# A planner's ranks and operation lengths set anew in a six-sublayer transformer kernel

## The chip, the cores and the metric

The kernel runs on one core of one Trainium2 chip. A core has five engines with a queue of instructions each: TensorE (PE: matrix products and transposes; PEld is its loading of the stationary operand), VectorE (DVE), ScalarE (ACT: functions from a table, and copies), GpSimd (POOL), and SyncE (SP), which here issues nearly all plain DMAs. Each engine works through its own queue strictly in order; semaphores tie the queues together. The metric is the device time of one execution in microseconds (us); less is better.

## The reference, cut to what matters

x is 16 sequences of 256 tokens with 128 channels. Two layers of one shape follow each other: half of an FFN, attention, half of the same FFN again.

```python
x = x + 0.5 * L0_ffn(layernorm(x))      # 8 experts of 128 -> 128 -> 128, top 2, SiLU gate, plus one shared expert
x = x + L0_attn(layernorm(x))           # 16 heads of 8; softmax(q1 k1) - lamb * softmax(q2 k2), then a layernorm
x = x + 0.5 * L0_ffn(layernorm(x))
x = x + 0.5 * L1_ffn(layernorm(x))      # 8 experts of 128 -> 256 -> 128, top 2, GELU gate
x = x + L1_attn(layernorm(x))           # 16 heads of 8, causal softmax, output projection
x = x + 0.5 * L1_ffn(layernorm(x))
```

Everything is float32.

## The kernel before

**Tiles.** The 4096 tokens are eight blocks of 512 (`x0` to `x7`), which stay on the chip from load to store. An FFN sublayer is done in parts of two blocks (the very last sublayer ends with two parts of one block each). The first two blocks of the first sublayer go through all experts densely (`dense_expert`), while the machinery of the sparse parts is set up; every other part is sparse. For a sparse part, `gate_block` normalizes and takes the gate, `dispatch` works out on DVE and PE which row goes to which slot, `scatter` writes the rows into `slots_x` in DRAM by indirect DMAs from POOL, `load_tiles` has SP fetch slots (`xg`) and expert weights (`wt`), `compute` does two tiles of 128 slots at a time, `combine` gathers the results `slots_y` by indirect DMAs into `g`, and `add_to_x` adds them on DVE.

**The chain of `compute`.** PE transposes `xg` into a PSUM half bank; ACT or DVE copies it to `xT`; PE multiplies by the first weights into a PSUM tile `big`; ACT applies SiLU or GELU with a bias, giving `s`; DVE multiplies, giving `h`; PE multiplies by the second weights; DVE adds a bias, giving `y`; SP stores `y`.

**Attention.** `Attention.pair` runs units: PE makes scores `big<-q,k`, ACT exponentiates them into `ex` (SiLU, GELU and Exp stand in different tables of ACT, and a change of table is an instruction of its own, ACT_TABLE_LOAD), in layer 1 DVE or POOL masks, PE sums `ex` with `vaug`, ACT copies `avs`, PE transposes it, DVE copies `oall`; `end` normalizes. PSUM has three `big` tiles and, once the dense work is over, four half banks.

**The order.** No engine's order is written by hand. Every piece of work is a generator that asks for an engine, with what it reads, writes and needs of buffers. A planner (`Tasks.run`) runs while the program is built. It keeps a model of time (`Clocks`), starts again and again the request whose modelled start plus `HASTE` (0.003) times its rank is least, and books a modelled length for each instruction (`Timed.book`). The order in which it starts requests becomes the order of PE, ACT, DVE and SP (`ORDERED`). So nothing but the orders follows from its numbers: the data, the shapes and the amount of PE work stay what they are. The same requests may fall to ACT or DVE (`move`) and, for masks, DVE or POOL (`MASKERS`).

**Its numbers.** `FFN_RANK` has a line for each FFN sublayer with a rank for each part; `ATT_RANK` a line for each attention sublayer with a rank for each block; a rank of 100 more is worth 0.3 us of modelled delay. `TABLE` (2.0 us) is added in the choice where ACT would have to change its table. `LATE_ROWS` is what `transfers` adds to the landing time of an indirect DMA (`s + 2.3 + LATE_ROWS`); consumers of `slots_x` and of `g` are planned after it. `Clocks.SEEN` adds 0.18 us between ACT's or DVE's end and another engine's start, 0.25 us after PE.

Nearly every instruction of the profile stands at L136, the line that records it (`f(*args, **kw)` in `Timed`), so groups are told apart by tiles. L1100 issues the scatters, L1258 the gathers. A choice at run time (`bounded`) takes the first of two programs with these inputs; the second, for large scores, is not run.

Of the kernel before, what the change touches and what calls it, by code (L numbers as in the profile page):

```python
# [24 lines left out]
SYNC = mybir.DependencyInfo(mybir.DependencyClass.Sync, mybir.DependencyReason.DATA)  # L25
TABLE = 2.0
LATE = 1.5
LATE_ROWS = 2.0
MARGIN = {"PE": 1.0, "ACT": 1.0, "DVE": 1.5, "POOL": 1.25, "SP": 2.0}
HASTE = 0.003  # L30

FFN_RANK = [
    [65, 53, 99],
    [190, 217, 235, 251],
    [218, 230, 258, 290],
    [420, 438, 430, 453, 403],
]
ATT_RANK = [
    [82, 122, 109, 110, 131, 132, 158, 159],
    [319, 320, 368, 341, 408, 369, 383, 574],  # L40
]


def cols(ap):
    n = 1
    for s in ap.shape[1:]:
        n *= s
    return n
# [6 lines left out]
class Clocks:  # L55
# [52 lines left out]
    def book(self, engine, length, reads, writes, by=None, end=None, start=None, apart=False):  # L108
        s = self.start(engine, reads, () if apart else writes)
        if start is not None:  # L110
            s = max(s, start)
        self.free[engine] = s + length
        end = s + length if end is None else end(s)
        by = by or engine
        for ap in reads:
            for k in self.keys(ap):
                self.read[k] = max(self.read.get(k, (0.0, by)), (end, by))
        for ap in writes:
            for k in self.keys(ap):
                self.wrote[k] = max(self.wrote.get(k, (0.0, by)), (end, by))  # L120
                if self.pending.get(k):
                    self.pending[k] -= 1
        return s


class Timed:
# [19 lines left out]
    def book(self, op, out, ins, args, kw):  # L146
        c, n = self.clocks, max(cols(v) for v in [out, *ins])
        if op == "dma_start":
            size = 4e-6 * n * out.shape[0]
            start = c.start("SP", ins, [out])  # L150

            def end(s):
                c.bytes_free = max(c.bytes_free, s + 1.2) + size / 0.3
                return max(s + 2.2, c.bytes_free + 1.0) + LATE

            c.book("SP", 0.45, ins, [out], by="DMA", end=end, start=start)
        elif self.name == "PE":
            turns = 1 if op == "transpose" or ins[0].dtype == BF else 2
            lanes = 4 if 32 in (out.shape[0], ins[0].shape[0]) else 1
            length = max(max(cols(out), 120) * 0.00094 / lanes, 0.0007 * cols(ins[0]))  # L160
            c.book("PE", turns * length + c.turn, ins, [out])
            c.turn = 0.0
        elif self.name == "ACT":
            func = args[2] if op == "activation" else None
            length = 0.16 + 0.00076 * cols(out)
            if func in (AF.Exp, AF.Silu, AF.Gelu) and func != c.table:
                c.table = func
                length += 1.3
            c.book("ACT", length, ins, [out])
        elif self.name == "DVE":  # L170
            c.book("DVE", 0.145 + 0.00097 * n, ins, [out])
        else:
            c.book("POOL", 0.35 + 0.17 * n if ALU.pow in args else 0.2 + 0.0021 * n, ins, [out])

# [78 lines left out]
def kernel(ctx: ExitStack, tc: tile.TileContext, a: dict, out: bass.AP):  # L253
# [690 lines left out]
    def transfers(todo, when=None, pool=None):  # L944
# [3 lines left out]
        for i in range(0, len(todo), 2):  # L948
# [3 lines left out]
            for j, (issue, _) in enumerate(two):  # L952
                start = clocks.start("POOL", reads)
                dma, ins, o = issue(taken[j] if pool else None)
                if clocks.last_before(start - 1.0) is not None:
                    tc.add_manual_dep(dma.ins, clocks.last_before(start - 1.0).ins.name, SYNC, reason="pace")
                clocks.book("POOL", 1.26, ins, [o], by="DMA", end=lambda s: s + 2.3 + LATE_ROWS, start=start, apart=True)

# [737 lines left out]
```

## Time and profile before

| what | value |
|---|---|
| median of 14 runs | 1536.83 us (1531.57 to 1544.52) |
| the profiled execution | 1524.25 us, of it the span 1522.5 us |
| PE busy | 1248.2 us, 82% of the span |
| PEld, DVE, ACT busy | 838.4, 888.1, 867.3 us (55%, 58%, 57%) |
| POOL busy | 609.6 us (40%) |
| mean granted clock of TensorE | 0.915 |
| HBM traffic | 155 GB/s over the span |

The profiled execution was 0.8% below the median. Busy shares are means over stages of different kinds: in the first 152 us (loads, dense experts, first dispatch) and the last 80 us (last FFN parts, last gathers and stores) PE has the most idle time; in between, FFN parts and attention blocks of different sublayers run beside each other. A "busy" PE may run at half rate; the granted clock tells of that. Where one row of the profile gives a mean for "one", that is from its start to its end; instructions of ACT and DVE that follow each other overlap in part, so several in a row take less than their number times the mean.

### The profile page before, as it was taken

To read this page: it belongs to the slowest core of one execution; us is meant where nothing else is said; L and a number is where in the kernel's file an instruction comes from. 1 tells how busy PE (TensorE), PEld (TensorE's weight loads), DVE (VectorE), ACT (ScalarE), POOL (GpSimd) and SP (SyncE) were. 2 spreads that over 40 slices of the span, in tenths; PEclk is the share of its full clock that TensorE was granted. 3 is DMA by queue.
4 is the path that set the end of the run, shared out by engine and by line. 5 is a ranking of instruction groups with operands and counts; after the bars stand their busy time and mean duration, and the time that the engine had idled before them with its cause. 6 is when DMAs were issued, how large, how long until landed. Compare 5 with 4: busy or idle time off the path is not lost. (4 is left out here: it accounts for less than half of the span.)

```text
span 1522.5 us, 29022 instructions
## 1 busy us (share of the span) xinstructions
PE 1248.2 (82%) x9730; PEld 838.4 (55%) x9730; DVE 888.1 (58%) x3146; ACT 867.3 (57%) x1612; POOL 609.6 (40%) x618
## 2 busy tenths in 40 slices
PE   5958889888898899888889877787878878887772
PEld 3434555554345444456665765476567756656772
DVE  4376734555535366554665676677665557766643
ACT  2114677677667676577678546464456655553431
POOL 2014442240530134424245364637553356475334
PEclk8858999999999999999999999799899989989986
DMA  5356555442125101357456554565355665446882
GB/s 116 96 131 193 181 163 159 148 141 81 49 84 143 32 19 41 116 177 249 139 154 187 188 174 133 179 223 191 136 188 162 204 204 176 138 171 209 269 289 86
DMA packets 207530, 232.85 MB, mean 153 GB/s; under 512 B 32062, under 2 KB 151545, under 8 KB 207371
## 3 DMA queue, kind: packets, MB, share of 16 engines
q1 hardware_dynamic: 192010, 199.42, 42.9%
q0 software_dynamic: 15360, 31.49, 6.3%
q8 instruction: 79, 1.29, 0.3%
q14 instruction: 81, 0.66, 0.1%
HBM read 183.84 MB, written 52.75 MB: 155 GB/s over the span
## 5 line engine op out<-in xcount | busy, mean ns | idle before, releaser
L136 ACT ACTIVATE ex<-big 128x1024 f32<-128x1024 f32 (+1 forms) x384 | 349.1, 958 | 81.5 <-PE big L136 66.6
L1100 POOL DMA_INDIRECT slots_x<-xn,idx x240 | 238.9, 995 | 256.4 <-PE bank L136 56.9
L1258 POOL DMA_INDIRECT g<-slots_y,idx x240 | 239.6, 999 | 241.2 <-PE big L136 61.5
L136 PE MATMUL big<-q,k 32*128 32x512 f32 (+1 forms) x1536 | 259.8, 635 | 14.0 <-ACT ex L136 3.6
L136 PE MATMUL big<-xT,wt 128*128 128x128 f32 x1452 | 205.4, 289 | 17.7 <-ACT xT L136 6.6
L136 ACT ACT_TABLE_LOAD x150 | 192.4, 1283 | 29.9 <-PE big L136 19.6
L136 PE MATMUL bank<-ex,vaug 128*32 128x256 f32 (+1 forms) x3072 | 190.0, 378 | 23.4 <-issue 10.1
L136 PEld LDWEIGHTS big<-xT,wt 128*128 128x128 f32 x1452 | 187.1, 202 | 33.5 <-issue 11.7
L136 POOL TENSOR_TENSOR rstd<-rstd,mhalf 128x4 f32<-128x4 f32 (+1 forms) x64 | 62.5, 977 | 310.7 <-DVE rstd L136 309.8
L136 PEld LDWEIGHTS bank<-ex,vaug 128*32 128x32 f32 x3072 | 92.7, 113 | 104.5 <-issue 37.2
L136 ACT ACTIVATE s<-big,wt 128x128 f32<-128x128 f32 x363 | 107.1, 374 | 67.0 <-PE big L136 34.5
L136 DVE SCALAR_TENSOR_TENSOR h<-big,wt,s 128x128 f32<-128x128 f32 x363 | 104.4, 342 | 60.0 <-ACT s L136 47.7
L136 PE MATMUL bank<-wt,h 128*128 128x128 f32 x726 | 120.2, 304 | 22.3 <-issue 6.6
L136 PEld LDWEIGHTS bank<-wt,h 128*128 128x128 f32 x726 | 102.3, 210 | 50.3 <-issue 17.8
L136 PEld LDWEIGHTS big<-q,k 32*128 32x128 f32 x1536 | 82.1, 193 | 83.8 <-issue 43.0
L136 PE MATMUL big<-xT,rw 128*128 128x128 f32 x720 | 113.7, 299 | 13.4 <-ACT ex L136 8.0
L136 DVE SCALAR_TENSOR_TENSOR x<-g,wgt,x 128x128 f32<-128x128 f32 x240 | 85.4, 360 | 53.0 <-DMA g<-slots_y,idx 40.3
L136 DVE COPY oall<-bank 128x144 f32<-128x144 f32 x96 | 29.2, 305 | 146.1 <-PE bank L136 92.7
L136 PEld LDWEIGHTS big<-xT,rw 128*128 128x128 f32 x720 | 101.5, 212 | 22.0 <-ACT ex L136 10.8
L136 ACT COPY avs<-bank 128x256 f32<-128x256 f32 x96 | 36.0, 375 | 132.4 <-PE bank L136 60.6
L136 DVE TENSOR_TENSOR y<-bank,wt 128x128 f32<-128x128 f32 x235 | 58.9, 284 | 86.4 <-PE bank L136 38.8
L136 ACT COPY xT<-bank 128x256 f32<-128x256 f32 (+1 forms) x184 | 63.2, 373 | 79.0 <-PE bank L136 49.1
(190 smaller groups left out, 1766.6 us busy)
## 6 DMA issues: line engine op xcount, KB each, us to landing
wt<-wcat SPq DMA_DIRECT2D x128, 450.0 KB
rw<-wcat SPq DMA_DIRECT2D x63, 450.0 KB
wt<-wcat SPq DMA_DIRECT2D x107, 257.0 KB
slots_y<-y SPq DMA_DIRECT2D x168, 128.0 KB
rw<-wcat SPq DMA_DIRECT2D x54, 257.0 KB
xg<-slots_x SPq DMA_DIRECT2D x43, 256.0 KB
cwb<-slots_x SPq DMA_DIRECT2D x33, 256.0 KB
slots_x<-zero SPq DMA_DIRECT2D x12, 384.0 KB
```

The lines of the kernel that those rows point to most:

```text
L136: r = f(*args, **kw)
L1100: s = bare.gpsimd.indirect_dma_start(out=self.sx[:, :], out_offset=bass.IndirectOffsetOnAxis(ap=self.idx[:, j, c : c + 1], axis=0), in_=ro ...
L1258: s = bare.gpsimd.indirect_dma_start(out=g[:, :], out_offset=None, in_=self.sy[:, :], in_offset=bass.IndirectOffsetOnAxis(ap=self.idx[:, j ...
```

## The change

Three things in the planner change, and nothing else:

```diff
-LATE_ROWS = 2.0
+LATE_ROWS = 2.5
 FFN_RANK = [
-    [65, 53, 99],
-    [190, 217, 235, 251],
-    [218, 230, 258, 290],
-    [420, 438, 430, 453, 403],
+    [65, 53, 101],
+    [190, 217, 235, 229],
+    [218, 230, 260, 290],
+    [420, 428, 420, 488, 450],
 ]
 ATT_RANK = [
-    [82, 122, 109, 110, 131, 132, 158, 159],
-    [319, 320, 368, 341, 408, 369, 383, 574],
+    [162, 192, 189, 65, 211, 212, 238, 154],
+    [312, 365, 366, 339, 398, 377, 382, 542],
 ]
...
         elif self.name == "ACT":
-            length = 0.16 + 0.00076 * cols(out)
+            length = max(0.25 if cols(out) > 64 else 0.15, 0.055 + 0.00084 * cols(out))
...
         elif self.name == "DVE":
-            c.book("DVE", 0.145 + 0.00097 * n, ins, [out])
+            if op == "reciprocal":
+                length = 0.05 + 0.0084 * n
+            else:
+                length = 0.085 + 0.001 * n + (0.05 if op in ("scalar_tensor_tensor", "bn_stats") else 0.0)
+            c.book("DVE", length, ins, [out])
```

The ranks change for both layers; the modelled length of ACT's copies and activations changes (a copy of 256 columns from 0.355 to 0.27 us), that of DVE's operations too (a tensor_tensor of 128 columns from 0.269 to 0.213 us, a reciprocal of 64 columns from 0.207 to 0.588 us); and indirect DMAs are taken to land 0.5 us later. The model of PE is left as it was.

## The prediction

> **What bounds the kernel now.** I read first the page's busy shares and slices, then the busy time by stage, then who ended the waits, then the groups.
>
> ```profile
> span 1522.5 us, 29022 instructions
> PE 1248.2 (82%) x9730; PEld 838.4 (55%) x9730; DVE 888.1 (58%) x3146; ACT 867.3 (57%) x1612; POOL 609.6 (40%) x618
> PEclk8858999999999999999999999799899989989986
> ```
>
> PE is busy 82% of the span, no other engine over 58%. PE idles 1522.5 - 1248.2 = 274 us; the stages (first 152 us: busy 109.84; from 1440 on, 82.5 us: busy 42.69) put 42 of it in the start and 40 in the end, and 192 in the 1288 us between. A second loss is the rate: by the clock's records TensorE had half rate for 258 us, 198 of them with PE busy; between 152 and 1440 that is 139 busy us, which at full rate would take half, so up to 69 us. The recorded rates are 0.5 and 1.0 only; the page's tenths are means.
>
> I cut PE's busy time into twentieths of 62.4 us of work each, and read the stages that these are:
>
> ```profile
> core 0: us, PE busy (x) PEld busy (x) DVE busy (x) ACT busy (x) POOL busy (x), PEclk, DMA share, GB/s
> 311.00:385.00 74.00, 62.86 (x511) 36.98 (x511) 44.11 (x158) 56.81 (x89) 23.55 (x25) 0.98 0.33 99
> 385.00:454.00 69.00, 62.16 (x564) 26.98 (x560) 28.95 (x100) 43.97 (x62) 31.57 (x33) 0.95 0.23 72
> 454.00:526.00 72.00, 62.63 (x522) 36.82 (x511) 33.71 (x108) 52.72 (x84) 4.46 (x5) 0.98 0.31 88
> 526.00:592.00 66.00, 62.53 (x572) 29.68 (x571) 43.24 (x161) 47.53 (x67) 23.95 (x25) 1.00 0.09 28
> 592.00:664.00 72.00, 62.57 (x477) 34.37 (x469) 38.40 (x134) 42.61 (x71) 29.86 (x31) 0.95 0.32 103
> 958.00:1038.00 80.00, 62.07 (x487) 48.92 (x484) 54.84 (x192) 43.19 (x93) 42.47 (x42) 0.87 0.64 201
> ```
>
> The same PE work takes 66 us where attention is nearly alone (526 to 592), and 80 where FFN parts, dispatch and attention are mixed (958 to 1038). So no single engine or transfer sets the middle; it is short waits of PE for ACT and DVE, whose number depends on the order:
>
> ```profile
> PE bank L136 <- ACT avs L136: 26.1, 20, 3.1
> PE bank L136 <- DVE y L136: 23.9, 24, 3.0
> PE bank L136 <- ACT xnT L136: 19.1, 25, 2.3
> PE big L136 <- ACT ex L136: 17.2, 20, 2.8
> PE bank L136 <- ACT xT L136: 11.5, 15, 2.7
> ```
>
> (us in total, times, longest.) The largest of these are one-copy hand-offs: PE, a copy on ACT, PE.
>
> **The change, part by part.** The two programs' orders on each engine were compared, instruction by instruction. Work is the same: PE 5258 recorded operations in both, SP 721 transfers in both, the same scatters and gathers; 3 of 485 ACT copies go to DVE, one mask from DVE to POOL (730 and 1330 ns: nothing, POOL is idle 60%). What differs is order, and with it the table loads. The change does not give the planner TensorE's half rate; the title's half rate went into the choice of ranks only, so the orders are still planned for full rate.
>
> (1) *Table loads.* The order of ACT has 150 in the program run before and 128 after.
>
> ```profile
> L136 ACT ACT_TABLE_LOAD x150 | 192.4, 1283 | 29.9 <-PE big L136 19.6 <-issue 7.1 <-PEq L1682 0.8
> ```
>
> 22 x 1283 ns = 28.2 us less on ACT. ACT is idle 43%, so most is hidden. From the start of a load to 1 us after its end PE idled 51.4 us over the 150, 0.34 us a load and no larger a share (15%) than elsewhere. Bounds: 0 and 22 x 0.34 = 7.5 us. I take 5, toward the full price, as these loads go where ACT is busiest (311 to 385: 56.81 of 74 us). Without the cover of ACT's idle time they would be worth all 28.2.
>
> (2) *Gathers planned 0.5 us later.* Until 1495 us, when the last gathers begin (their 16 at 1.26 us each follow in both orders alike: block 7's eight, then block 6's), DVE stood at the head of its queue for a gather:
>
> ```profile
> DVE x L136 <- DMA g<-slots_y,idx: 24.4, 24, 2.3
> ```
>
> 24 waits x 0.5 = 12 us of DVE at best. What stands behind is whatever DVE has next (y, h, oall); PEld waited 5.5 us, 6 times, for these additions. Bounds 0 and 5.5; I take 2, by the PE waits' half that 0.5 us of a wait's mean 1.0 us removes, less some for work that now comes after.
>
> (3) *Right lengths.* Rows and timeline: an ACT copy of 256 takes 382 ns alone, two in a row 0.65 us, so the next starts 0.27 us later; before it was planned as 0.355, now 0.27. Of DVE, two y additions take 0.49 us, 0.21 us apart (planned 0.269, now 0.213); a reciprocal of 64 columns 552 ns (0.207, now 0.588). The new numbers are the trace's. PE waited for ACT's avs, xnT, xT (twice, 11.5 and 8.2 us) and k 86 times, 73 us: 86 x 0.085 = 7.3 us, and for y 24 x 0.056 = 1.3 us, if every consumer moves up by the error: bounds 0 and 8.6. I take 4, half, since a consumer moves up only where nothing else was put before it.
>
> ```profile
> L136 ACT ACTIVATE s<-big,wt 128x128 f32<-128x128 f32 x363 | 107.1, 374 | 67.0 <-PE big L136 34.5 <-issue 13.8 <-PE bank L136 12.1
> L136 ACT COPY xT<-bank 128x256 f32<-128x256 f32 x168 | 59.9, 382 | 78.5 <-PE bank L136 48.9 <-issue 12.2 <-DVE y L136 6.5
> ```
>
> Four activations of 128 take 1.14 us, 0.255 each in a row against 374 alone. [...]
>
> (4) *Regrouped layer 0.* Attention of layer 0 is moved by ranks 70 to 80 later, blocks 3 and 7 excepted. In the orders, with each PE operation weighted by its row's busy time, twentieths 5 to 9 (20% to 45%) held 34, 31, 28, 34, 25 Exp and 12, 8, 16, 1, 18 SiLU; now 40, 34, 35, 27, 32 Exp and 0, 1, 8, 17, 4 SiLU. Before, two of the five had under 10 SiLU (385 to 454 and 526 to 592: PE idle 6.8 and 3.5 us, mean 5.2), the other three 11.1, 9.4 and 9.4 (mean 10.0). Now four are of the quiet kind: 2 x 4.8 = 9.6 us, 16 if all four become like the best (40.2 before, 4 x 3.5 + 10.0 after). SP's fetches, POOL's gathers and the FFN work move with it to 45% to 60%: the price of that is in (5). Bounds 0 and 16; I take 10.
>
> (5) *Closer hand-offs.* For each PE step that waits on ACT or DVE I took the PE work that stands between it and the PE step that feeds its chain, the queues' order included. Under 2 us: 303 steps before, 351 after; under 1 us: 105 and 117. Of the 48 more, 24 lie between 45% and 60% of PE's work; the second products (`bank<-h`) rise most, and behind one stand an activation and a multiplication (1.14 and 1.12 us). Over the 18 twentieths between the ends, PE's idle time in the trace grows by 0.39 us with each hand-off under 2 us, or by 0.82 with each under 1 (correlations 0.58 and 0.61). 47 x 0.39 = 18.3 (one of the 48 is in the first twentieth) or 12 x 0.82 = 9.8. Bounds 0 and 18.3; I take 10, since (3) says that part of the slack given up was never needed.
>
> Idle PE also lowers the rate. Between 152 and 1440 us half rate costs up to 69 us beside 192 idle, 0.36 for each us idle; on the net sum that is under 4 us, left in the range. TensorE: Matmul & The Clock Gate (HAM oscillation) has the rule "no PE-idle gaps >~3.4µs": by it waits of at most 2 us cost no rate. Before its last matmul the trace has four stretches that long, one of them past 152 us, and between 152 and 1440 us 147 us of half rate; the measurement decides.
>
> Sum: -5 - 2 - 4 - 10 + 10 = -11 us on the profiled execution's 1524.25, 1513. That one lay 12.6 us below the median of the runs, so the forecast is put on the median: 1536.8 - 11 = 1526 us.
>
> **The rivals.** *The closer hand-offs decide (slower).* Place: 45% to 60% of PE's work, where FFN parts of both layers now meet. If regrouping only carries idle time there, (4) is 0, and (5) is 18.3; with 5 for the table loads, and (2) and (3) lost in the same waits, +13, 1550 us. It decides from a price of 11 / 47 = 0.23 us a hand-off when (4) is 0. For it: the 0.39 of the twentieths, and that 877 to 1114 is already the worst stretch; against it: a copy needs under 1 us, so most hand-offs of 1 to 2 us fit. *All terms at their good end.* -7.5 - 5.5 - 8.6 - 16 = -37.6, half of it with (5) at half (9) gives about -28, with the rate 1507 us. For it: 69 us of half rate and 192 idle to take from; against it: from the second layer's attention on the order of stages is nearly the old one (each begins and ends within 2% of PE's work). *Hidden.* The waits change places and the total stays: 1537 us. For it: start, end and half the middle are nearly unchanged.
>
> **How the numbers follow.** Forecast (1517 to 1532) 0.34, the good end 0.19, no change 0.13, slower 0.34. About 0.3%, 4.6 us, is what a measurement can tell. Faster 0.53, same 0.13, slower 0.34. The bounds, -37.6 and +18.3, are 1499 and 1555; the range that leaves two in ten out is 1502 to 1553. My own range for the forecast alone is 1517 to 1532.
>
> **What would show it.** 128 table loads (if not, (1) falls); gather waits of DVE before the last gathers under 15 us; PE waits for avs, xnT, xT under 60 us in place of 65; PE idle between 20% and 45% of its work near 30 us in place of 40; between 45% and 60% not above 40 (it was 26). If that last stretch gains more than 20 us of idle time, or the mean clock falls below 0.90, the forecast is wrong.

## The result, and the profile after

The changed kernel takes 1596.96 us (median of 10 runs, 1588.64 to 1602.47) against 1535.36 us for the kernel before (47 runs), a ratio of 1.0398 (95% interval 1.0375 to 1.0422). It is slower by 4%. The forecast was 1526 us, and the range ended at 1553. The profiled execution took 1582.8 us, of it 1581.1 us span, 58.6 us more than the span before.

The page of the kernel after, with the busy time of each engine and the granted clock by slices:

```profile
span 1581.1 us, 28975 instructions
PE 1266.0 (80%) x9730; PEld 846.3 (54%) x9730; DVE 891.6 (56%) x3148; ACT 839.9 (53%) x1587; POOL 608.4 (38%) x619
PEclk8859999999999999999998987899889999979986
```

The work is the same 9730 products. PE idles 315.1 us in place of 274.3 (+40.8), and is busy 17.8 us longer: it had half rate for 236 busy us in place of 198, and half of those 38 extra us is the 17.8 to within about a microsecond. So 40.8 of idle time and 17.8 of rate make up the 58.6. ACT is busy 27 us less and DVE 3.5 us more; no engine has become the bound. The table loads are the 128 that were read off the orders:

```profile
L136 ACT ACT_TABLE_LOAD x128 | 164.2, 1283 | 30.4 <-PE big L136 13.7
```

Next the waits of the kernel after (us in total, times, longest), those of PE that answer to the ones shown of before, and DVE's wait for gathers:

```profile
DVE x L136 <- DMA g<-slots_y,idx: 55.5, 51, 6.0
PE bank L136 <- DVE y L136: 37.6, 29, 4.6
PE bank L136 <- DVE h L136: 25.2, 17, 6.2
PE big L136 <- ACT ex L136: 19.8, 24, 2.5
PE bank L136 <- ACT avs L136: 18.4, 15, 4.4
PE bank L136 <- ACT xnT L136: 16.8, 23, 2.6
PE bank L136 <- ACT xT L136: 14.9, 18, 2.3
```

and from the same view of the kernel before one row that the prediction did not show:

```profile
PE bank L136 <- DVE h L136: 7.6, 7, 1.7
```

PE's waits for ACT, summed over all rows of PE's own view, stay at 99 us (before 100). Those for DVE grow from 88 to 137 us, +49, which is more than all the added idle time. The two rows to look at are `y` (23.9 to 37.6) and `h` (7.6 to 25.2): the two DVE steps of the expert chain, with longest waits now of 4.6 and 6.2 us where none was over 3.0.

Where in the run? Cut into twentieths of PE's work (by the weighted orders, as in (4) of the prediction), with PE's idle time beside, the stages changed their length so:

| share of PE's work | longer by, us | idle before, after |
|---|---|---|
| 0 to 10% | -3.9 | 46.7, 47.3 |
| 10 to 20% | +21.5 | 15.3, 28.8 |
| 20 to 35% | -21.5 | 28.1, 13.7 |
| 35 to 45% | +9.6 | 11.6, 19.9 |
| 45 to 60% | +25.1 | 24.7, 42.3 |
| 60 to 80% | +20.0 | 63.1, 74.4 |
| 80 to 100% | +8.0 | 84.8, 88.9 |

The view of windows of the kernel after shows both sides: two of the quiet stages, then the stretch at 50 to 60% of the work, where FFN parts of both layers now meet.

```profile
core 0: us, PE busy (x) PEld busy (x) DVE busy (x) ACT busy (x) POOL busy (x), PEclk, DMA share, GB/s
403.00:463.00 60.00, 57.13 (x528) 24.71 (x528) 30.29 (x93) 44.41 (x62) 5.30 (x6) 1.00 0.00 1
463.00:524.00 61.00, 57.09 (x527) 25.97 (x519) 26.45 (x83) 44.30 (x60) 17.30 (x18) 1.00 0.20 66
735.00:809.00 74.00, 60.52 (x485) 47.23 (x488) 41.81 (x173) 46.21 (x90) 33.28 (x35) 0.95 0.67 211
809.00:894.00 85.00, 66.21 (x499) 42.63 (x497) 44.44 (x158) 47.84 (x87) 47.37 (x49) 0.88 0.55 170
```

The kernel before had these windows for the same shares of the work as the last two:

```profile
726.00:797.00 71.00, 62.18 (x489) 44.38 (x481) 47.94 (x190) 49.27 (x90) 22.45 (x24) 0.93 0.47 142
797.00:864.00 67.00, 59.59 (x530) 40.77 (x527) 40.44 (x143) 48.00 (x85) 29.34 (x29) 0.97 0.70 216
```

A twentieth of the work is 57 us at full clock, so the first two are near the best there can be; the stretch from 809 on takes 85 us where 67 did, at a clock of 0.88 in place of 0.97, with DVE and ACT busy about half of it. It lacks no engine and no bandwidth; things wait in line.

How a closer hand-off costs PE its time can be seen in one place. The timeline of the kernel after (start, duration, engine, and in brackets the idle time before and who ended it), PE first:

```profile
185.82 0.75 PE L136 MATMUL bank<-wt,h 128*128 128x128 f32 x4
186.40 1.88 PE L136 MATMUL big<-xnT,sw 128*128 128x512 f32 x4
192.83 1.22 PE L136 MATMUL bank<-sw,h 128*128 128x128 f32 x4 [4.55 <-DVE y L136]
```

and ACT and DVE in the same stretch:

```profile
190.30 0.69 ACT L136 ACTIVATE s<-big,b_0t 128x512 f32<-128x512 f32 x1
189.68 0.31 DVE L136 COPY oall<-bank 128x144 f32<-128x144 f32 x1 [2.27 <-PE big L136]
189.91 0.74 DVE L136 SCALAR_TENSOR_TENSOR h<-big,b_0t,s 128x512 f32<-128x512 f32 x1
190.57 0.68 DVE L136 TENSOR_TENSOR x<-x,sb 128x512 f32<-128x512 f32 x1
191.17 0.42 DVE L136 TENSOR_TENSOR eq<-lg 128x256 f32<-128x256 f32 x1
191.62 0.42 DVE L136 TENSOR_TENSOR eq<-eq,earlier 128x256 f32<-128x256 f32 x1
191.96 0.42 DVE L136 TENSOR_TENSOR gt<-lg 128x256 f32<-128x256 f32 x1
192.30 0.48 DVE L136 TENSOR_TENSOR y<-bank,wt 128x128 f32<-128x128 f32 x2
```

The product that stands, a second product of the shared expert (`bank<-sw,h`), does not wait for the first one just ahead of it (`big<-xnT,sw`): that one's activation only begins at 190.30, and the `h` that the waiting product reads is from an earlier one and is ready at 190.65. By its program it waits for `y`, which has to read the result of `bank<-wt,h` (185.82) out of the same PSUM bank. Between `bank<-wt,h` and the product that needs its `y` done, PE has 1.88 us of work of its own. DVE is idle until 189.68, and then has a copy, a multiplication for `h`, an addition to `x` and three comparisons of `dispatch` ahead of that `y`. PE stands 4.55 us. In the kernel before, this second product never waited more than 1.24 us; its three groups around 185 us stood behind score products or a dispatch product, which gave PE something to do.

### The profile page after: what moved, and what is told of

Its sections match the earlier page's. It is cut to its first block, busy times and chain, and to the rows that moved or that the text cites. A ratio compares the mean times of both kernels' runs of the same rounds, so it can differ in the third digit from the quotient of the medians.

```text
span 1581.1 us, 28975 instructions
## 1 busy us (share of the span) xinstructions
PE 1266.0 (80%) x9730; PEld 846.3 (54%) x9730; DVE 891.6 (56%) x3148; ACT 839.9 (53%) x1587; POOL 608.4 (38%) x619
## 5 line engine op out<-in xcount | busy, mean ns | idle before, releaser
L1262 POOL DMA_INDIRECT g<-slots_y,idx x240 | 235.4, 981 | 230.6 <-PE bank L136 99.6
L136 PE MATMUL big<-xT,wt 128*128 128x128 f32 x1460 | 215.4, 295 | 21.5 <-ACT ex L136 10.0
L136 PEld LDWEIGHTS big<-xT,wt 128*128 128x128 f32 x1460 | 196.4, 209 | 39.5 <-issue 15.3
L136 POOL TENSOR_TENSOR rstd<-rstd,mhalf 128x4 f32<-128x4 f32 (+1 forms) x64 | 63.3, 988 | 330.1 <-DVE rstd L136 328.9
L136 ACT ACT_TABLE_LOAD x128 | 164.2, 1283 | 30.4 <-PE big L136 13.7
L136 PE MATMUL bank<-wt,h 128*128 128x128 f32 x730 | 124.8, 307 | 29.7 <-issue 8.1
L136 PEld LDWEIGHTS bank<-wt,h 128*128 128x128 f32 x730 | 105.5, 212 | 56.8 <-issue 19.0
L136 DVE SCALAR_TENSOR_TENSOR x<-g,wgt,x 128x128 f32<-128x128 f32 x240 | 89.2, 377 | 63.3 <-DMA g<-slots_y,idx 55.5
L136 POOL TENSOR_TENSOR ex<-ex,causal 128x512 f32<-128x512 f32 x48 | 61.9, 1310 | 105.4 <-ACT ex L136 105.3
```

The source lines that it names most:

```text
L136: r = f(*args, **kw)
L1262: s = bare.gpsimd.indirect_dma_start(out=g[:, :], out_offset=None, in_=self.sy[:, :], in_offset=bass.IndirectOffsetOnAxis(ap=self.idx[:, j ...
```

## The experiments

Three sets of numbers changed (ranks, lengths, `LATE_ROWS`), so the first runs took them apart. The theories, by the letters used in the expectations: A, the new ranks are the cause; B, the new, mostly shorter lengths place each consumer too close behind its producer; C, the order before is one that was selected, and any other order that the planner makes loses (C': loses only on some chips); D, the time follows the count of close hand-offs, that is, of PE steps with under 2 us of PE work between them and the step that feeds their chain (before 303, after 351); E, the new lengths of DVE are shorter than the true ones; F, the fewer table loads are bought with late activations.

The runs were spread over five sessions. In two of them, as in the first comparison, the kernel before took 1536 to 1539 us; in the other three, 1438 to 1441. Ratios are each to the kernel before beside it; the two settings are taken up in the last section. The first four expectations give times for a kernel before of 1535 us, but their session had 1441: only their ratios can be compared.

**One part at a time.** e1_ranks takes only the rank tables of the change, e2_lengths only the lengths of ACT and DVE, e3_late only `LATE_ROWS`, e4_ranks_lengths all but `LATE_ROWS`. Of each part a line, in the order e3, e2, e1:

```diff
-LATE_ROWS = 2.0
+LATE_ROWS = 2.5
...
-            length = 0.16 + 0.00076 * cols(out)
+            length = max(0.25 if cols(out) > 64 else 0.15, 0.055 + 0.00084 * cols(out))
...
-    [82, 122, 109, 110, 131, 132, 158, 159],
+    [162, 192, 189, 65, 211, 212, 238, 154],
```

> The new ranks alone; lengths and the landing time of indirect DMAs as before. The whole change took 61.6 us more at the median (1535.4 to 1597.0). Theory A (ranks were fitted to the new lengths and regroup layer 0 badly; they are the cause): 1580 to 1610 us. Theory B (the shorter planned lengths make the planner place consumers too close; ranks are harmless): 1525 to 1545 us. Theory C (any new order loses, since the old one is a lucky one among many): 1550 to 1590 us, and the lengths alone as much.

> The new lengths of ACT and DVE alone, old ranks. Theory A: 1525 to 1545 us. Theory B: 1580 to 1610 us, with more waits of PE for DVE's h and y than before. Theory C: 1550 to 1590 us.

> Indirect DMAs planned 0.5 us later alone. Theories A and B: 1525 to 1545 us, no difference from before. Theory C: even this small step, which reorders only what stands near a scatter or a gather, loses 10 us or more: 1545 to 1590 us.

> The whole change but for the later landing of indirect DMAs. Theories A and B: within 10 us of the whole change, 1587 to 1607 us. Theory C: anywhere between 1550 and 1600 us, not predictable from the parts.

| kernel | median us | ratio, 95% interval | close hand-offs | table loads |
|---|---|---|---|---|
| before | 1440.98 | 1 | 303 | 150 |
| e1_ranks | 1486.27 | 1.031, 1.026 to 1.037 | 340 | 143 |
| e2_lengths | 1520.79 | 1.054, 1.047 to 1.060 | 365 | 135 |
| e3_late | 1474.08 | 1.023, 1.018 to 1.028 | 331 | 156 |
| e4_ranks_lengths | 1592.35 | 1.106, 1.098 to 1.115 | 387 | 124 |

Every part loses by itself, and the loss grows with the count of close hand-offs. Neither A nor B alone can be the cause: a change of one constant that only delays modelled gathers (e3) loses 2.3%. That asked for a neutral change.

**Neutral changes.** c1_before is the kernel before under another name, c2_after the whole change; n1_haste_up and n2_haste_down alter only the weight of all ranks by 3%, to 0.0031 and 0.0029:

```diff
-HASTE = 0.003
+HASTE = 0.0031
```

> The kernel before, unchanged, for its profile on the same chip as the others of this call. The chip of the last four runs took 1441 us for it and the chips before it 1535. All theories: ratio 1.00. If the time is near 1440 again, its profile shows which instructions, waits or transfers are shorter than in the 1522.5 us profile.

> The whole change, unchanged, on the same chip as the kernel before. Theory C' (the loss of a new order is specific to the chip): the ratio differs clearly from the first comparison's 1.040, and lies near 1.10 on a chip where the kernel before takes 1440 us. Theories A and B: 1.04 on any chip.

> A neutral reshuffle: HASTE 0.0031 in place of 0.003, all else as before. The planner's lengths and ranks are unchanged and the weight of rank grows by 3%, so no theory of a better or worse model predicts anything: A and B 0.995 to 1.005. C (the order before is a lucky one, any reshuffle loses): 1.01 to 1.04.

> The opposite neutral reshuffle: HASTE 0.0029; the first 1600 rows or so of TensorE's order stay as before. A and B: 0.995 to 1.005. C: 1.01 to 1.03.

Beside 1536.43 us: c1_before 1.000 (0.996 to 1.004), c2_after 1.034 (1.027 to 1.041), n1_haste_up 1.020 (1.013 to 1.026), n2_haste_down 1.013 (1.007 to 1.019). A nudge in either direction, which has no better or worse side, costs 1.3 to 2.0%: theory C holds on another chip too (and the whole change, with 1.034, is near the first 1.040, so C' falls for this setting). But the whole change costs more than a nudge, and it is there that PE's waits for DVE rise: all rows together 96 us in c1_before, 92 and 103 in the two nudges, 134 in c2_after.

**The count by itself.** If D is the rule, ranks chosen for the count alone must do well or badly. o1_fewer moves nine ranks of the kernel before so as to have 288 close hand-offs; o2_after_fewer moves twelve ranks of the changed one and has 311 in place of 351; d1_more is o1 with four other ranks (468, 460, 371, and 225 for 217) and has 375; n3_late_down has `LATE_ROWS` at 1.9, and 330. Most of o1's moves:

```diff
-    [420, 438, 430, 453, 403],
+    [420, 453, 445, 453, 433],
-    [319, 320, 368, 341, 408, 369, 383, 574],
+    [319, 320, 369, 341, 423, 367, 383, 604],
```

> Lengths and landing time as before; ten ranks moved, chosen by the order alone so that fewer TensorE steps have under 2 us of TensorE work between them and the step that feeds their chain: 288 in place of 303 (under 3 us: 594 for 603). Theory D (the time follows the number of close hand-offs at 0.6 to 1.3 us each, as in the seven orders run so far): 10 to 20 us faster, ratio 0.987 to 0.994. Theory C (the order before was chosen on the chip among many, and the count only happens to follow): slower, 1.01 to 1.03, like any other reshuffle.

> The whole change with its own lengths and landing time, but ten ranks moved so that 311 hand-offs are under 2 us in place of 351 (under 3 us: 639 for 664); 124 table loads of this kind of order stay few. Theory D: 25 to 50 us faster than the whole change, ratio to before 1.005 to 1.02. Theory B (the shorter lengths themselves hurt) and C: 1.03 to 1.05, no better than the whole change.

> Four ranks away from the first kernel of this call, lengths and landing time as before, about as many table loads (143), but 375 hand-offs under 2 us (under 3 us: 660). Theory D: 45 to 95 us slower than before, ratio 1.03 to 1.06, as bad as the whole change or worse although planner and lengths are the old ones. Theory C: 1.01 to 1.03.

> Indirect DMAs planned to land 0.1 us earlier, all else as before: 330 hand-offs under 2 us (27 more), 597 under 3 us (6 fewer). Theory D with 2 us as the measure: 16 to 35 us slower, ratio 1.01 to 1.023. With 3 us as the measure: 0.99 to 1.00. Theory C: 1.01 to 1.03.

Beside 1438.23 us: o1_fewer 1.014 (1.010 to 1.018), o2_after_fewer 1.047 (1.042 to 1.051), d1_more 1.067 (1.062 to 1.073), n3_late_down 1.049 (1.044 to 1.054). The count tells the bad order (d1, 77 us above o1 with 87 hand-offs more, 0.9 us each), but does not lead below the kernel before: with 15 fewer than that, o1 is still 1.4% slower, and o2 and n3 cost far more than their 8 and 27 more would have.

**DVE's lengths.** The waits for DVE pointed to theory E. f1_act has only ACT's new lengths, f2_dve only DVE's, f3_no_dve all of the change but DVE's lengths, c4_after the whole change. The lines that f2 has and f3 lacks:

```diff
-            c.book("DVE", 0.145 + 0.00097 * n, ins, [out])
+            if op == "reciprocal":
+                length = 0.05 + 0.0084 * n
+            else:
+                length = 0.085 + 0.001 * n + (0.05 if op in ("scalar_tensor_tensor", "bn_stats") else 0.0)
+            c.book("DVE", length, ins, [out])
```

> Only ACT's new lengths; ranks, DVE's lengths and LATE_ROWS as before. 367 hand-offs with under 2 us of PE work between (before 303), 123 table loads. Theory E (DVE's new planned lengths are shorter than its pitches in the trace, so DVE's results come late and PE waits for them): DVE's lengths are untouched, so PE's waits for DVE stay within 15 us of the other reshuffles at the same setting of the machine (about 87 to 105 us), ratio 1.01 to 1.03. Theory D (the count decides, 1.2 us each): 64 more, 77 us, ratio 1.05. Theory C (any other order loses): 1.013 to 1.067 like the others, with no place for the loss.

> Only DVE's new lengths; ranks, ACT's lengths and LATE_ROWS as before. 343 hand-offs under 2 us, 126 table loads. Theory E: PE's waits for DVE rise by 25 us or more over f1_act on the same chip, above all for y and h, and the ratio is at least 1.015 above that of f1_act. Theory D: 40 more, 48 us, ratio 1.03, below f1_act. Theory C: 1.013 to 1.067 with no order between f1_act and f2_dve.

> The whole change without DVE's new lengths (new ranks, ACT's lengths, LATE_ROWS 2.5). 354 hand-offs under 2 us (the whole change 351), 132 table loads. Theory E: faster than the whole change by 1.5% or more on the same chip, PE's waits for DVE 25 us or more below the whole change's. Theory D: like the whole change, within 0.7%. Theory C: anywhere between 1.013 and 1.067, no tie to DVE's waits.

> The whole change once more, as the reference for f3_no_dve on this chip. At the setting in which the kernel before takes about 1536 us: ratio 1.034 to 1.040 as measured twice. At the setting in which it takes about 1440 us, where the profiles have next to no waits of PE for nothing, theory C gives the same ratio, theory E a larger one (1.05 to 1.10), as there only the waits for DVE and ACT are left to set the time.

Beside 1538.70 us: f1_act 1.052 (1.046 to 1.058), f2_dve 1.031 (1.025 to 1.036), f3_no_dve 1.042 (1.036 to 1.048), c4_after 1.038 (1.032 to 1.043). E has f2 above f1 and f3 well below c4; it is the other way round, and theory D had 1.05, 1.03 and "like the whole change, within 0.7%", which came true in all three. PE's waits for DVE, all rows, are 139 us in f1_act and 142 in f2_dve, where E had 25 more in f2_dve. From the waits of f1_act:

```profile
PE bank L136 <- DVE h L136: 48.0, 17, 10.8
PE bank L136 <- DVE y L136: 27.8, 21, 3.7
```

of f2_dve:

```profile
PE bank L136 <- DVE h L136: 42.4, 21, 6.4
PE bank L136 <- DVE y L136: 24.3, 23, 5.0
```

and of c4_after:

```profile
PE bank L136 <- DVE y L136: 45.1, 34, 4.5
PE bank L136 <- DVE h L136: 23.1, 14, 5.8
```

With DVE's own lengths untouched (f1), PE's waits for `h` are the largest of all. So E falls. That DVE ends so many waits does not mean that DVE is planned wrongly: `h` is the last step of a chain of three engines (PE, ACT, DVE), so a delay anywhere in the chain can show up there.

**Table loads.** Orders with few table loads had the long waits for `h` (f1 124 loads, f2 127, the change 128). F was tried by making a change of table cheap to the planner, in the changed kernel (g1) and in the kernel before (g2):

```diff
-TABLE = 2.0
+TABLE = 0.8
```

> The whole change with TABLE 0.8 in place of 2.0, so that the planner changes ACT's table sooner: 157 table loads (the whole change 128, the kernel before 150), 361 hand-offs with under 2 us of PE work between (the whole change 351, before 303). Theory F (fewer loads are bought with activations that stand at ACT behind another function's run, and PE then waits for the products h that need them): PE's waits for h fall from 32 to 35 us to under 25, and the ratio falls to 1.02 or less, although ACT works 37 us more on loads than in the whole change. Theory D (the count of close hand-offs at 1.2 us each): 58 more than before, ratio 1.045, no better than the whole change. Theory C (any other order loses, no single cause): 1.013 to 1.067.

> The kernel before with TABLE 0.8 alone: 169 table loads, 286 close hand-offs (303 before). Theory F: PE's waits for h not above those of the kernel before (12 to 17 us), ratio 0.99 to 1.01. Theory D: 17 hand-offs fewer at 1.2 us, ratio 0.987, faster than the kernel before. Theory C: slower than before by 1.3% or more, as every other order so far.

Beside 1439.85 us: g1_after_cheap_table 1.058 (1.054 to 1.062), g2_before_cheap_table 1.027 (1.023 to 1.030). With 157 loads and nearly the change's count of close hand-offs (361 against 351), g1 waits for `h` no less than the change does (25.2 us in the same row, in the other setting):

```profile
PE bank L136 <- DVE h L136: 34.3, 23, 5.8
PE bank L136 <- DVE y L136: 29.2, 28, 3.2
```

F falls; D had 1.045, too little. And g2, with 286 close hand-offs, is slower than the kernel before, so D, by this count, fails below 303 a second time.

**What the runs say together.** In the setting with 1536 us, f1, f2 and f3 cost 1.2, 1.1 and 1.2 us for each close hand-off above the 303 of the kernel before, and the whole change, at the mean of its three ratios (+57 us), 1.2. In the setting with 1440 us, a straight line through the ten orders rises 0.90 us with each close hand-off, but at 303 the line stands at +37 us, and points lie 20 us off it (root mean square). Much hangs on how one counts. Taken from the semaphores of the programs, with the work of the feeding step itself included, the kernel before has 313 and each of the sixteen orders has more, o1 with 322 the fewest, g2 with 340. So it is not shown that an order with fewer close hand-offs would be no faster. And by this count the whole change has 350, n1 371 and n2 345, where the two nudges cost 32 and 21 us and the change 57: the count goes with the loss and does not set it, and what sets the change off from a nudge stays open. None of the sixteen orders measured beats the kernel before; no version better than both was found.

## Why the prediction was wrong

**The step that failed** is (5), the price of a closer hand-off. Its bounds were 0 and 0.39 us each, and the sum took 10 us for 47 (0.21 each). In the runs that take the change apart in its own setting (f1, f2, f3) each one above 303 goes with 1.1 to 1.2 us; 48 of them make 53 to 58 us, and 57 were measured. That is what goes with a closer hand-off in these orders; a price that each one pays is not shown, as the nudges tell. There were two reasons for the small figure. The 0.39 was a slope within one trace, from twentieth to twentieth, with a correlation of 0.58, which leaves two thirds of the variation to other things; what another order of the same work costs is not to be had from it. And it counted idle time alone. The added 40.8 us of idle time alone are 0.85 for each of the 48. The rest is rate: 17.8 us for 40.8 idle, 0.44 for each us. The prediction had worked out 0.36 for each us, then applied it to a net sum near zero and dropped it. The ratio was near; what it was applied to was not.

How short waits cost rate can be read off the trace. Between 152 and 1440 us, TensorE had half rate for 193 us (before 147), in 38 stretches (before 32) that last 3.41 us or a whole multiple of it. Only six of them (before one) have a stretch of 3.4 us or more without a product in the 4 us ahead. What nearly all have is short idle time: PE idled 2.3 us of these 4 at the median (before 2.0), where 0.4 (before 0.3) is the median over that whole part of the run. The Trainium skill has a passage that fits this better than the rule of long gaps which the prediction set against the trace: TensorE: Matmul & The Clock Gate (A second HAM failure mode: psum-queue depth-cycling) tells of another kernel, in bf16, in which PE idles briefly between groups of matmuls, often enough that the clock swings between half and full.

**The baseline.** The sum was made against zero: what the change does to the named terms, and nothing else. The runs show that an order with no such terms, n1 or n2, is 1.3 to 2.0% slower already, and each of the sixteen other orders is. This was in no term and no rival. Whether the kernel before holds its place because its ranks were searched on the chip can't be read from the runs; that its neighbours are worse is shown.

**(1) Table loads.** 128, as forecast. From the start of a load to 1 us after it, PE idled 56.6 us over 128 loads (0.44 each; before 51.4 over 150, 0.34). That is 19% of that time, about what PE idles anywhere (20%). Neither a gain nor, by g1, a loss can be seen.

**(2) Gathers planned later.** The waits before the last gathers should have fallen under 15 us. These begin at 1553 us now, and until then DVE waited 39.3 us, 35 times, against 24.4, 24 times; over the whole run it is 55.5 against 40.3. What `LATE_ROWS` does by itself stays open: e3 has 63.3 us over its run, the least of the ten orders profiled in the setting with 1440 us (the others 71.6 to 109.4), but the kernel before was not profiled in it.

**(3) Right lengths.** Waits for avs, xnT and xT are 58.1 us in place of 64.9, within the forecast of under 60 (6.8 less, where 4 was taken for these with k and y; y rose by 13.7). But a shorter booking does not only move the consumer of one copy up; it lets the planner draw chains closer together. ACT's lengths alone have 367 close hand-offs, and cost 5.2%. So "the new numbers are the trace's" was true of the copies and was no argument: the old, longer bookings were wrong as lengths, and the order made with them keeps more distance.

**(4) Regrouped layer 0.** The gain is there: 20 to 45% of PE's work is 11.9 us shorter. Of idle time, which the forecast of 10 was made of, it is 6.1 us (from 39.7 to 33.6, near 30 forecast); the rest is rate. It was given back at once: the two twentieths before it, from which the timeline above is, are 21.5 us longer, and 45 to 60% is 25.1 longer.

**The rival** named the right place. The stretch at 45 to 60% went from 24.7 to 42.3 us idle, past the mark of 40; but that stretch is 25 of the 58.6 us. The 877 to 1114 us that the prediction had for the rival are 60 to 75% of the work by its own twentieths, not this place; and the -28 of its good end is all of -37.6 with the 9 of (5), not half of it. The other twentieths beyond 60%, which the prediction took as nearly unchanged because the stages begin and end where they did, lost 28 us more (20.0 and 8.0). The same stages in the same place are not the same order inside.

## What to carry to other kernels

Before summing what a reordering should bring, ask what a reordering that means nothing costs: here two runs with a nudged constant cost 1.3 and 2.0%, more than the whole forecast gain. Where one planner sets all queues, count for each step of the bound engine how much of its own work stands between it and the step that feeds its chain; here every order with more close hand-offs than the kernel before was slower, however right its lengths. Whether one with fewer would be faster was not settled. A wait is charged to the engine that ends it, which may be only the last step of a chain, so try that engine's part alone before mending it.

## What the runs showed of the hardware

The same kernel before took 1536 to 1539 us in two sessions and 1438 to 1441 us in three, and two chips gave both. Within a session all its runs lay within 1.4%. One visible trace of the difference is the stretches in which PE waited for nothing that the profile shows ("issue" in the view of waits). In c1_before, of the setting with 1536 us:

```profile
PE bank L136 <- issue: 23.9, 27, 3.3
PE big L136 <- issue: 9.0, 17, 1.4
```

In o1_fewer, of the setting with 1440 us, this is the only such row:

```profile
PE bank L136 <- issue: 0.5, 1, 0.5
```

Over all kernels it is 33 to 55 us in the first setting and 0 to 3 us in the second. For the kernel before it is 45 and 33 us in its two profiles, a third to a half of the 96 us. The granted clock differs too: over the runs of the kernel before it is 0.908 at the mean in the two sessions of the first setting, and 0.929 in the three of the second. The durations of like rows of ACT, DVE and POOL do not (the median of their ratios between c1_before and o1_fewer is 1.00). What the rest is, and what sets the setting, stays open. The kernel before was not profiled in the second setting, and the whole change was not timed there; e4, which lacks only `LATE_ROWS`, was 1.106 there, so the whole change may well lose more in it than the 3.4 to 4.0% that three comparisons in the first setting show.
